# Four-layer graph network on one core: layer 2's last two gating tiles one by one, its last ELU from PSUM, W1 in halves, row exponentials and layer 3's score turns later

## The chip, the cores and the metric

The kernel runs on one core of one Trainium2 chip. The metric is device time in microseconds of one launch, the median of several runs, so less is better. A core has five engines, each with its own instruction queue, taken in order: TensorE (PE in the profile, its weight loads PEld), VectorE (DVE), ScalarE (ACT), GpSimd (POOL) and SyncE (SP), which here issues most of the DMAs. Engines wait for each other through semaphores. All data is float32. Each float32 product with a full tile shows up in the profile as two matmul records, a transposition as one.

## The reference, cut to what matters

x is 2708 x 256, adj is 2708 x 2708. Four layers each add a graph step and a feed-forward step to x. What the change touches lies in layer 2 and at the start of layer 3:

```python
# layer 2, graph step on xn = layernorm(x)
h = xn @ W.T
a_src = (h * attn_src).sum(-1);  a_dst = (h * attn_dst).sum(-1)
scores = a_src[None, :] + a_dst[:, None]
s = where(scores > 0, scores, 0.2 * scores) * mask          # mask = adj > 0
e = exp(s - max(s, axis=1)) * mask
x = x + elu(e / (sum(e, axis=1) + 1e-8) @ h)
# layer 2, feed-forward step on xn = layernorm(x)
logits = mean(xn, over all rows) @ Wr + br                  # one routing for all rows
weights = softmax(softmax(logits) * scale);  top 2 of 8 experts, softmax of the two
y = sum over the two experts of w_e * (gelu(xn @ W1[e] + b1[e]) @ W2[e] + b2[e])
x = x + layernorm(y + xn) * gamma + beta
# layer 3, graph step: four heads, score_l and score_r of xn @ W.T, softmax over neighbours
```

Since the routing of layer 2 depends on the mean over all rows, no expert can be chosen, and none of its weights loaded, before the last row's graph step is done.

## The kernel before, in words

The 2708 rows are 22 tiles of 128 rows, the last (number 21, `FULL`) with only 20. x stays in SBUF as `x[:, t, :]`. Eight PSUM banks have two roles in this part: three for short-lived results (`ps_tmp`) and five for accumulators (`ps_acc`); a new tile of a role waits until the one that had its bank is read.

**Layer 2's front** (lines 1570 to 1685) goes through the groups of tiles in `FOURS` (2, 4, 4, 4, 4, 4 tiles). `turned_up` adds what the layer before left in DRAM (`mine`, loaded by SP; added on DVE, from tile 14 on on POOL, line 1588), turns the tiles (PE, line 1596) and copies them to `xT4` (ACT, line 1598). `valued` multiplies with W and the two attention vectors (PE, line 267), copies the scores (ACT, line 1639) and puts `hh`, the scaled values, and exponentials of the scores. The scores along the row have to reach all partitions: `row_scores` turns them (PE, line 1497), copies them (ACT, line 1499) and writes them to DRAM (SP, line 1500); `row_factor` reads them back, broadcast to 128 partitions (SP, line 1504), and takes their exponential in place (ACT, `lnexp`, line 141). Since ACT's queue is in order, everything behind this exponential waits for the round trip through DRAM.

**Gating** (lines 1736 to 1782). The loop goes over batches of 5, 5, 5, 4 and 2 destination tiles. For each source tile j, one DVE instruction (line 1745) makes the weights `e` for all the batch's tiles, in one of four buffers; then PE adds `e.T @ hh[j]` to each tile's accumulator (line 1753; the 20 rows of tile 21 by `last_product`, line 313). Column 256 of `hh` yields the sum of weights. When a batch is through, `result` (line 1690) adds `rowe` to the sum, takes the reciprocal (DVE) and copies the scaled accumulator to `o` (ACT, line 1696). `grow` takes the ELU (relu and exponential on ACT, lines 1702 and 141; two additions on DVE, 1704 and 1705), and row statistics (DVE, 1707 and 1708; Ln and Exp on ACT). `turned` normalises to `xn` (ACT, 1717), turns it into `xnT` (PE, 1721), and its copies also sum the columns into `xsum` (ACT, 1726). These closings of a batch are handed out within the next batch's loop, one at every second j (line 1755).

**Routing** (lines 1786 to 1852). After the last batch of two tiles, PE adds bias and the column sums of the other 20 tiles to the logits, `grow` is run on the two tiles, and their share is added as a weighted sum (line 1798: x times the reciprocal deviation, one column). Then a chain of small DVE and ACT instructions picks two experts and their weights, and the two tiles are turned.

**Feed-forward** (lines 1912 to 2055). SP reads the experts' numbers from `ix`, and loads their W1 (128 x 2 x 512 each) and W2. Six parts of 512, 512, 512, 512, 384 and 276 rows follow: `units` makes the hidden layer of both experts (PE line 375, gelu on ACT line 377), `finish` normalises the part before, `outputs` multiplies with W2 (PE, line 1962), and `front` does layer 3's front for the part before: turn, project (line 267), copy values and scores (ACT, lines 2015 to 2018), and at its end turn the scores (`row_scores`, PE line 1497) and write them to DRAM. Layer 3's gating reads them later.

**What sets the order.** The program is written in the order of the source, and a scheduler then orders each engine's queue by its own estimate of times; `engine_after` and `after` add order by hand, tying an engine's instructions from one place on behind a named one. Each engine then runs its queue in that order.

Of the kernel before, what the change touches and what calls it, by code (L numbers as in the profile page):

```python
# [8 lines left out]
F32 = mybir.dt.float32  # L9
# [6 lines left out]
P = 128  # L16
N = 2708
D = 256
# [48 lines left out]
def adj_ffn4(ctx: ExitStack, tc: tile.TileContext, a: dict, out: bass.AP):  # L67
# [1438 lines left out]

    def row_factor(dst, kept, h, t0, n):

        row_read(dst, kept, h, t0, n)
        lnexp(dst, dst, AF.Exp, scale=0.8)  # L1510


# [4 lines left out]
    with tc.tile_pool(name="t3", reuse_waits="tile", bufs=1) as t3:  # L1517
# [25 lines left out]

        SUMMED = NT - 2
        xsum = tp.tile([P, DC, SUMMED], F32, name="xsum")

# [5 lines left out]
        with tc.tile_pool(name="g2", reuse_waits="tile", bufs=1) as gp:  # L1552
# [3 lines left out]
            Rb = gp.tile([P, NT * P], F32, name="Rb")  # L1556
            kept = tc.dram_tile([NT, 1, P], F32, name="rows2")

            fronts = (mybir.EngineType.PE, mybir.EngineType.DVE, mybir.EngineType.Activation)
# [10 lines left out]
            def turned_up(tiles):  # L1570

                n, t0 = len(tiles), tiles[0]
                adder = v if t0 < FOURS[4][0] else g
                xT = gp.tile([P, DC, W], F32, name="xT4", bufs=2)
                late = [t for t in tiles if t not in EARLY]
                if late:
                    o = gp.tile([P, 4, D], F32, name="mine", bufs=2)
                    for i in load_tiles(nc, o, late, given[1], t0):
                        behind(i, scattered["given1"])
# [46 lines left out]
            def scores_of(tiles):  # L1626
                sc = gp.tile([P, 4, 2], F32, name="sc", bufs=2)
                (v if tiles[0] < FOURS[2][0] else g).memset(sc, 0.0)
                return sc, []
# [26 lines left out]

            ahead, todo = [turned_up(FOURS[0])], list(FOURS[1:])
            for k in range(len(FOURS)):
                sc, t0, n = valued(*ahead.pop(0))
# [23 lines left out]
                if k > 0:  # L1683
                    row_scores(kept, sc[:, :n, 1], t0, n)
                row_factor(Rb[:, t0 * P : (t0 + n) * P], kept, 0, t0, n)

# [12 lines left out]
            def grow(t, q, o):  # L1699

                e = work.tile([P, D], F32, name="elu_e")[:q]
                s.activation(e, o, AF.Relu, scale=-1.0)
                lnexp(e, e, AF.Exp, scale=-1.0)
                v.scalar_tensor_tensor(x[:q, t, :], o, 0.0, x[:q, t, :], op0=ALU.max, op1=ALU.add)
                v.scalar_tensor_tensor(x[:q, t, :], e, -1.0, x[:q, t, :], op0=ALU.add, op1=ALU.add)
                st = small.tile([P, 6], F32, name="st")
                v.bn_stats(st[:q], x[:q, t, :])
                v.bn_aggr(mrs[:q, t, :], st[:q])
                lnexp(mrs[:q, t, 1:2], mrs[:q, t, 1:2], AF.Ln, bias=eps[:q])
                lnexp(mrs[:q, t, 1:2], mrs[:q, t, 1:2], AF.Exp, scale=-0.5)  # L1710
# [25 lines left out]
            t0, seen, todo = 0, 0, []  # L1736
            for n in (5, 5, 5, 4, 2):
                own = [(t, (t - t0) * P, P) for t in range(t0, t0 + n)]
                c0, w = t0 * P, n * P
                t0 += n  # L1740
                acc = [ps_acc() for _ in own]
                for j in range(NT):
                    r = P
                    e = gp.tile([P, 5 * P], F32, name="e", bufs=4)
                    i = v.scalar_tensor_tensor(e[:r, :w], Rb[:r, c0 : c0 + w], G[:r, j, :],  # L1745
                                           mask[:r, j, c0 : c0 + w], op0=ALU.max, op1=ALU.mult)
                    if c0 == 0 and j == 12:
                        spread = i.ins.name
                    for n, ((t, k, q), p) in enumerate(zip(own, acc)):
                        if j == FULL:  # L1750
                            last_product(p[:, : D + 1], n % 4, e, k, hh[:, FULL, :])
                        else:
                            te.matmul(p[:, : D + 1], lhsT=e[:, k : k + q], rhs=hh[:, j, :],  # L1753
                                      start=(j == 0), stop=False)
                    if j % 2 and j > 2 and todo:
                        todo.pop(0)()
                made = [result(t, q, p) for (t, k, q), p in zip(own, acc)]
                if c0 == 0:
# [14 lines left out]
                        ps_tmp(), es, lambda j, r: hh[:r, j, :], D + 1)))  # L1773
                if t0 == FULL:
                    break
                for it in made:
# [13 lines left out]
            for c in range(DC):  # L1790
                te.matmul(logits, lhsT=xb[:, c : c + 1].to_broadcast([P, P]), rhs=wr[:, c, :],
                          start=False, stop=False)
            for it in made:
                grow(*it)
            p = ps_tmp()
            for i, (t, q, _) in enumerate(made):
                for c in range(DC):
                    te.matmul(p[:, c : c + 1], lhsT=x[:q, t, c * P : (c + 1) * P],
                              rhs=mrs[:q, t, 1:2], start=(i + c == 0),
                              stop=(i == len(made) - 1 and c == DC - 1))  # L1800
            xb = gp.tile([P, DC], F32, name="xb", bufs=2)
# [48 lines left out]
            v.tensor_tensor(wts[:, 1, :], wts[:, 1, :], wts[:, 0, :], ALU.mult)  # L1850
            for it in made:
                turned(*it[:2])

# [58 lines left out]
        with tc.tile_pool(name="h2", reuse_waits="tile", bufs=2) as hp:  # L1912
# [4 lines left out]
            b1s = hp.tile([P, 2, H2C], F32, name="b1s", bufs=1)  # L1917
            chosen = [nc.values_load(ix[0:1, k : k + 1], engines=[mybir.EngineType.SP], min_val=0,
                                     max_val=E - 1,
                                     skip_runtime_bounds_check_because="the index of a one-hot's one")  # L1920
                      for k in range(2)]
            for k, e in enumerate(chosen):
                nc.sync.dma_start(w1[:, k], a["L2_ffn_W1"][bass.ds(e, 1)].rearrange(
                    "e (c p) h -> p (e c) h", p=P))
            for k, e in enumerate(chosen):
# [103 lines left out]

            was = None  # L2030

            parts = CHUNKS[:-2] + [(CHUNKS[-2][0], 3 * P), (CHUNKS[-2][0] + 3 * P, W + CHUNKS[-1][1] - 3 * P)]
            for c0, w in parts:
                own = tiles_of(c0, w)
                end = c0 + w == N
                hT, i = units(c0, w)
                if end:


                    pin(i.ins.name)  # L2040
                    rows_of(0, "both")
                    last_mask()
                    factors(0, was[0][0][0])
                if was is not None:
                    at_once(finish(*was, end))
                y = ypool.tile([P, 4, D], F32, name="y", bufs=2)
                outputs(own, hT, y)
                if was is not None:
                    at_once(front(was[0]))
                    for t in range(NT) if was[0][0][0] == 0 else ():  # L2050
                        r = rows(t)
                        g.tensor_copy(mask[:, t, t * P : t * P + r], diag[:, t, :r])
                if end:
                    factors(was[0][0][0], own[0][0])
                was = (own, y)
# [262 lines left out]
```

## Time and profile before

| | us |
|---|---|
| median of three runs (1900.36 to 1915.36) | 1911.79 |
| the profiled execution's own time | 1882.29 |
| its span in the profile | 1880.6 |
| PE busy in the span | 1820.4 |
| DVE busy | 1076.1 |
| ACT busy | 656.0 |
| POOL busy | 387.3 |
| mean clock granted to PE, share of full | 0.985 |

By stage, in us from the span's start: layer 2's front from about 1063 to 1095, its gating from 1095 to 1308.5, the routing to 1324, the feed-forward step to 1508, layer 3 to the end. In a line of the timeline the first number is the start, the second the duration (of all where x says more than one), then engine, source line, operation, what is written and from what, the shape, and in brackets how long the engine stood idle before and what ended that. A line of the waits gives engine and line, who released it, the total in us, how often and the longest. Durations are those of one execution.

### The profile page before, as it was taken

How to read it: one execution, taken by the hardware profiler on the slowest of the kernel's cores; microseconds unless marked ns; L12 is line 12 of the kernel's file. 1: busy time of each engine (PE TensorE's matmuls, PEld its weight loads, DVE VectorE, ACT ScalarE, POOL GpSimd, SP SyncE). 2: the span in 40 equal slices, each digit the busy share in tenths (PEclk: the TensorE clock that was granted, in tenths of full speed). 3: DMA queues.
4: the chain of work that ended last, by engine and by line, in shares of the span. 5: the costliest groups of instructions: out<-in, count | busy, mean ns of one | idle time of the engine just before them, and what ended most of it. 6: DMA issues, size and time to landing. Idle time of an engine off the chain costs nothing. (4 is left out here: it accounts for less than half of the span.)

```text
span 1880.6 us, 25848 instructions
## 1 busy us (share of the span) xinstructions
PE 1820.4 (97%) x9453; PEld 1335.0 (71%) x9453; DVE 1076.1 (57%) x2468; ACT 656.0 (35%) x1474; POOL 387.3 (21%) x460
## 2 busy tenths in 40 slices
PE   8999999999999999999999899998899999999998
PEld 7888788888888888888788788887566733233344
DVE  7687863444333525354642465555445498888877
ACT  8868742222222303113232323223223551132232
POOL 0014254333331001403547310000000100011020
PEclk9999999999998999999999999999899999999999
DMA  8535657877873554544775430000101000022120
GB/s 269 157 104 161 225 177 283 336 301 281 305 272 108 165 150 119 146 113 130 218 235 166 140 70 7 1 1 1 45 1 34 18 1 24 23 28 35 26 35 18
DMA packets 92494, 231.63 MB, mean 123 GB/s; under 512 B 18207, under 2 KB 48967, under 8 KB 84936
## 3 DMA queue, kind: packets, MB, share of 16 engines
q1 hardware_dynamic: 70792, 183.28, 29.8%
q0 software_dynamic: 21568, 46.61, 8.9%
q8 instruction: 78, 1.28, 0.3%
q14 instruction: 56, 0.46, 0.1%
HBM read 218.39 MB, written 30.80 MB: 133 GB/s over the span
## 5 line engine op out<-in xcount | busy, mean ns | idle before, releaser
L2190 DVE SCALAR_TENSOR_TENSOR e<-arena,G,mask 128x1024 f32<-128x1024 f32 (+1 forms) x252 | 275.1, 1151 | 34.1 <-PE den L2227 33.2
L2219 PE MATMUL num<-e,wh 128*64 128x512 f32 (+4 forms) x1056 | 214.1, 549 | 0.7 <-ACT L_gnn_W L1499 0.3
L1753 PE MATMUL ps_acc<-hh,e 128*128 128x257 f32 x882 | 199.2, 382 | 1.7 <-ACT o L1696 1.7
L1025 PE MATMUL acc<-msg,wt 128*128 128x256 f32 x882 | 197.8, 381 | 1.5 <-DVE wt L975 1.2
L1421 PE MATMUL acc<-sup,adrow 128*128 128x256 f32 x882 | 198.3, 382 | 0.7 <-DMA adrow<-in_adjT 0.4
L1421 PEld LDWEIGHTS acc<-sup,adrow 128*128 128x128 f32 x882 | 165.1, 190 | 28.4 <-issue 5.5
L1753 PEld LDWEIGHTS ps_acc<-hh,e 128*128 128x128 f32 x882 | 164.0, 191 | 29.0 <-ACT o L1696 4.3
L1025 PEld LDWEIGHTS acc<-msg,wt 128*128 128x128 f32 x882 | 165.5, 191 | 26.7 <-DVE wt L975 1.8
L615 PE MATMUL ps_acc<-xTs,wa 128*128 128x256 f32 (+1 forms) x768 | 169.9, 374 | 2.8 <-DVE xTs L605 2.7
L617 ACT ACTIVATE hTs<-ps_acc,wa 128x256 f32<-128x256 f32 (+1 forms) x192 | 88.8, 464 | 237.7 <-PE yacc L649 155.6
L649 PE MATMUL yacc<-wb,hTs 128*128 128x256 f32 x736 | 170.6, 384 | 0.1
L615 PEld LDWEIGHTS ps_acc<-xTs,wa 128*128 128x128 f32 x768 | 137.2, 191 | 29.0 <-DVE xTs L605 5.1
L2219 PEld LDWEIGHTS num<-e,wh 128*64 128x64 f32 (+1 forms) x1056 | 70.2, 136 | 122.7 <-issue 105.4
L649 PEld LDWEIGHTS yacc<-wb,hTs 128*128 128x128 f32 x736 | 138.8, 192 | 18.1 <-DVE ys L651 0.5
L1745 DVE SCALAR_TENSOR_TENSOR e<-Rb,G,mask 128x640 f32<-128x640 f32 (+2 forms) x110 | 85.0, 774 | 90.5 <-PE ps_acc L1753 90.4
L1386 DVE TENSOR_SCALAR mask<-adrow 128x1024 uint8<-128x1024 f32 (+1 forms) x66 | 41.6, 630 | 124.1 <-DMA adrow<-in_adjT 123.7
L2227 PE MATMUL den<-e,wh 128*32 128x512 f32 (+4 forms) x1056 | 112.2, 546 | 0.0
L221 ACT COPY xT<-ps_tmp 128x256 f32<-128x256 f32 x76 | 26.8, 366 | 199.1 <-PE ps_tmp L220 198.7
L782 PE MATMUL yacc<-wb,hTs 128*128 128x256 f32 x384 | 90.0, 390 | 0.0
L975 DVE SCALAR_TENSOR_TENSOR wt<-adrow,wt 128x640 f32<-128x640 f32 (+3 forms) x67 | 71.2, 1065 | 25.1 <-ACT wt L141 24.8
L2227 PEld LDWEIGHTS den<-e,wh 128*32 128x32 f32 (+1 forms) x1056 | 33.2, 109 | 73.6 <-issue 69.5
L537 POOL DMA_INDIRECT given<-ys,xs x46 | 65.3, 1420 | 84.0 <-DVE ys L652 68.2
(487 smaller groups left out, 2632.6 us busy)
## 6 DMA issues: line engine op xcount, KB each, us to landing
adhalf<-in_adjT SPq DMA_DIRECT2D x42, 677.0 KB
wb<-in_L_ffn_W2p SPq DMA_DIRECT2D x24, 1152.0 KB
wb<-in_L_ffn_Wdp SPq DMA_DIRECT2D x24, 1152.0 KB
wa<-in_L_ffn_W1b SPq DMA_DIRECT2D x24, 1028.0 KB
adrow<-in_adjT SPq DMA_DIRECT2D x42, 512.0 KB
adrow<-in_adjT SPq DMA_DIRECT2D x42, 320.0 KB
adrow<-in_adjT SPq DMA_DIRECT2D x21, 576.0 KB
adrow<-in_adjT SPq DMA_DIRECT2D x21, 448.0 KB
```

The costliest lines, as they stand in the source:

```text
L615: i = te.matmul(p[:, f % 2, : m * P], lhsT=w1[:, c, f * P : (f + 1) * P], rhs=xT[:, c, : m * P], start=(c == 0), stop=(c == DC - 1))
L617: s.activation(hT[:, f, : m * P], p[:, f % 2, : m * P], AF.Gelu, bias=bias[:, f : f + 1])
L649: te.matmul(q[:, k, :], lhsT=hT[:, f, k * P : (k + 1) * P], rhs=w2[:, f, :], start=(f == 0), stop=(f == HC - 1))
L782: te.matmul(q, lhsT=hT[:, f, :], rhs=w2[:, f, :], start=(f == 0), stop=(f == HC - 1))
L975: v.scalar_tensor_tensor(wt, ad, 1.0, wt, op0=ALU.is_lt, op1=ALU.mult)
L1025: te.matmul(p[:q, n - pair[0], :], lhsT=wt[:, k : k + q], rhs=msg[:r, j, :], start=(j == 0 and n == pair[0]), stop=(j == FULL - 1 and n == ...
L1421: te.matmul(p[:q, n - pair[0], :], lhsT=ad[:, k : k + q], rhs=sup[:, jj, :], start=(jj == 0 and n == pair[0]), stop=(jj == FULL - 1 and n ...
L1745: i = v.scalar_tensor_tensor(e[:r, :w], Rb[:r, c0 : c0 + w], G[:r, j, :], mask[:r, j, c0 : c0 + w], op0=ALU.max, op1=ALU.mult)
L1753: te.matmul(p[:, : D + 1], lhsT=e[:, k : k + q], rhs=hh[:, j, :], start=(j == 0), stop=False)
L2190: v.scalar_tensor_tensor(e[:, :w], slow[:, m % 2, k, :w], G[:, j, 2 * pair + k, :], mask[:, j, c0 : c0 + w], op0=ALU.max, op1=ALU.mult)
L2219: te.matmul(num[k * DK : (k + 1) * DK, hf, :q], lhsT=wh[some, j, 2 * pair + k, :DK], rhs=e[some, :q], start=(j == 0), stop=(j == FULL), ti ...
L2227: te.matmul(den[z * Q : (z + 1) * Q, :q], lhsT=wh[some, i, 2 * pair + k, DK : DK + 1] .to_broadcast([some.stop - some.start, Q]), rhs=e[so ...
```

## The change

- The row exponential is taken one group later: `row_factor` is gone; after the next group's `row_scores`, `factors_of` takes the exponential of the group before, tied behind ACT's last instruction.
- The buffers of the front get a pool of their own, which is closed after the front; its room goes to 22 kept tiles of weights `e_last` (128 x 256).
- The batches are 5, 5, 5, 4, 1 and 1. The weights of both single tiles are made in one instruction for each source tile: 18 of them within the four-tile batch, four right after it. The single passes read them; closings are handed out at j = 4, 9, 14 and 19 of a single pass.
- `SUMMED` is 21: only the last full tile (20) is added to the mean by the weighted sum.
- The last tile's ELU reads the accumulator in PSUM: the sum and reciprocal are taken with a minus sign, ACT's relu scales with it, and DVE takes min(-v, 0) and subtracts it from x. The rest of `grow` is now `normed_by`.
- The first expert's W1 is loaded in two halves of 256 columns, with the second expert's number read after them.
- A part's last step of `front`, the turn of the scores, is emitted after the next part's `units`, with PE tied behind its last product; the last part's is run at once.

```diff
-    def row_factor(dst, kept, h, t0, n):
-        row_read(dst, kept, h, t0, n)
-        lnexp(dst, dst, AF.Exp, scale=0.8)
...
-        SUMMED = NT - 2
+        SUMMED = NT - 1
...
+            def factors_of(dst):
+                had, first = last_of(fronts), len(nc.cur_bb.bb.instructions)
+                lnexp(dst, dst, AF.Exp, scale=0.8)
+                engine_after(first, mybir.EngineType.Activation, had[mybir.EngineType.Activation])
...
-                row_factor(Rb[:, t0 * P : (t0 + n) * P], kept, 0, t0, n)
+                for f in factor:
+                    factors_of(f)
+                factor = [Rb[:, t0 * P : (t0 + n) * P]]
+                row_read(factor[0], kept, 0, t0, n)
+            factors_of(factor[0])
...
+            def weigh_last():
+                both_last.append(pair_pool.tile([P, 2 * P], F32, name="e_last", bufs=NT))
+                return weigh(both_last[-1], len(both_last) - 1, PAIR * P, 2 * P)
...
-            for n in (5, 5, 5, 4, 2):
+            for n in (5, 5, 5, 4, 1, 1):
+                single = t0 - PAIR
...
+                    if single >= 0:
+                        if len(both_last) < NT and single == 0:
+                            weigh_last()
+                        e = both_last[j]
+                    else:
+                        e = gp.tile([P, 5 * P], F32, name="e", bufs=4)
+                        i = weigh(e, j, c0, w)
+                        if t0 == PAIR and j > 3:
+                            after(weigh_last(), i.ins.name)
...
-                    if j % 2 and j > 2 and todo:
+                    if (j in (4, 9, 14, 19) if single >= 0 else j % 2 and j > 2) and todo:
                         todo.pop(0)()
...
-            for it in made:
-                grow(*it)
+            t, p = FULL - 1, acc[0]
+            rs = small.tile([P, 1], F32, name="rs")
+            v.scalar_tensor_tensor(rs, p[:, D : D + 1], -1.0, rowe[:, t, :], op0=ALU.mult,
+                                   op1=ALU.subtract)
+            v.reciprocal(rs, rs)
+            e = work.tile([P, D], F32, name="elu_e")
+            s.activation(e, p[:, :D], AF.Relu, scale=rs)
+            lnexp(e, e, AF.Exp, scale=-1.0)
+            o = gp.tile([P, D], F32, name="o", bufs=6)
+            v.tensor_scalar(o, p[:, :D], rs, 0.0, op0=ALU.mult, op1=ALU.min)
+            v.tensor_tensor(x[:, t, :], x[:, t, :], o, ALU.subtract)
+            normed_by(t, P, e)
...
+                for h0 in ((0, H2 // 2) if k == 0 else (0,)):
+                    h1 = H2 if k else h0 + H2 // 2
+                    nc.sync.dma_start(w1[:, k, :, h0:h1], a["L2_ffn_W1"][bass.ds(e, 1), :, h0:h1]
+                                      .rearrange("e (c p) h -> p (e c) h", p=P))
...
                 hT, i = units(c0, w)
+                if scored is not None:
...
+                    at_once(scored)
+                    engine_after(at, mybir.EngineType.PE, done)
+                    scored = None
...
-                    at_once(front(was[0]))
+                    scored = front(was[0])
+                    for _ in range(len(was[0]) + 1):
+                        next(scored)
+                    if end:
+                        at_once(scored)
```

## The prediction

> **What bounds the kernel now.** I read the page's busy shares first, then TensorE's waits, then the timeline of each place that the diff touches.
>
> ```profile
> PE 1820.4 (97%) x9453; PEld 1335.0 (71%) x9453; DVE 1076.1 (57%) x2468; ACT 656.0 (35%) x1474; POOL 387.3 (21%) x460
> ```
> TensorE (PE) is the bound nearly everywhere: 1880.6 - 1820.4 = 60 us of the span are left for all its idle time. The change removes no sizeable PE work, so it can win only parts of that idle time. Who ends it (line, releaser, total us, times, longest):
>
> ```profile
> PE ps_tmp L1497 <- issue: 5.1, 5, 1.1
> PE ps_tmp L1798 <- ACT mrs L141: 4.0, 1, 4.0
> ...
> PE ps_tmp L1596 <- ACT xT L1598: 3.4, 1, 3.4
> ...
> PE ps_acc L1753 <- ACT o L1696: 1.7, 3, 0.8
> ...
> PE ps_tmp L375 <- DMA w<-in_L_ffn_W: 0.8, 1, 0.8
> ...
> PE ps_tmp L1721 <- ACT xn L1717: 0.6, 1, 0.6
> ```
> These six are the waits that the edits aim at. The first is named "issue", but the timeline (start, duration, engine, line) shows that the turn of the scores starts when ScalarE (ACT) has written the last of them:
>
> ```profile
> 1384.01 2.24 PE L267 MATMUL ps_tmp<-w_l,xT 128*128 128x264 f32 x8
> 1387.00 0.28 ACT L2018 ACTIVATE sc<-ps_tmp,rs_y 128x4 f32<-128x4 f32 x1
> 1387.39 0.27 PE L1497 MATMUL ps_tmp<-ident,sc 128*16 128x128 f32 x1 [1.14 <-issue]
> ```
> In layer 2's front, ACT stands 4.29 us for a row's round trip through DRAM, and PE then lacks the copies queued behind it; GpSimd's (POOL's) two adds run in the same gap:
>
> ```profile
> 1076.42 2.48 POOL L1588 TENSOR_TENSOR x<-x,mine 128x512 f32<-128x512 f32 x2 [6.61 <-DMA mine<-given]
> 1076.76 0.42 ACT L141 ACTIVATE Rb<-Rb 128x256 f32<-128x256 f32 x1 [4.29 <-DMA Rb<-rows]
> ...
> 1079.33 1.09 PE L1596 MATMUL ps_tmp<-ident,x 128*128 128x128 f32 x4 [3.36 <-ACT xT L1598]
> ```
> After the last gating product a chain over two tiles runs with PE idle:
>
> ```profile
> 1308.69 0.16 DVE L1693 TENSOR_TENSOR rs<-ps_acc,rowe 128x1 f32<-128x1 f32 x1 [2.75 <-PE ps_acc L313]
> 1310.92 1.03 DVE L1705 SCALAR_TENSOR_TENSOR x<-elu_e,x 128x256 f32<-128x256 f32 x2 [0.16 <-ACT elu_e L141]
> 1313.36 1.86 PE L1798 MATMUL ps_tmp<-mrs,x 128*128 128x1 f32 x8 [4.04 <-ACT mrs L141]
> 1324.04 1.19 PE L375 MATMUL ps_tmp<-arena,w 128*128 128x512 f32 x1 [0.82 <-DMA w<-in_L_ffn_W]
> ```
> The windows by time (us, then busy time by engine, third number from the end the clock granted to PE) show a second price of a long gap:
>
> ```profile
> 1074.00:1076.00 2.00, 1.91 (x12) 1.03 (x10) 2.00 (x7) 0.00 (x0) 0.00 (x0) 1.00 0.80 255
> 1079.30:1080.30 1.00, 0.97 (x5) 1.00 (x6) 1.00 (x3) 0.52 (x2) 0.00 (x0) 0.50 0.36 39
> 1084.30:1085.30 1.00, 1.00 (x4) 0.86 (x3) 0.12 (x1) 0.26 (x1) 0.77 (x3) 0.65 0.61 117
> ```
> The clock is halved after the 3.36 us gap, and whole again only some 5 us into steady work.
>
> **What the Trainium skill says.** "TensorE: Matmul & The Clock Gate", section "The HAM clock gate": an idle window of about 3.4 us halves PE's clock, about as long a busy one restores it, and the window runs free. The trace agrees in kind: gaps of 0.6 to 1.2 us leave the clock whole, one of 1.75 (at 253.3) too, but those of 2.10 (at 1036.1) and 2.26 (at 992.3) already halve it. "PSUM — Partial Sum Buffer", section "PSUM bank collisions raise a hardware error": ScalarE and VectorE may not read one bank at once. This decides a step below: in the changed program VectorE's (DVE's) read of the accumulator waits for ACT's, so the two reads add. The trace of before has no such pair. [...]Here 512 KB of W1 took 4.1 us from issue (1319.92) to the product that waits for it (1324.04), and nearly nothing moved in its first two us.
>
> **The change part by part**, against the profiled execution: span 1880.6, its own time 1882.29; the runs' median is 1911.79 (1900.36 to 1915.36), so the profiled execution was 1.5% quicker than the median. The difference in us is carried over.
>
> (e) Four of layer 3's five score turns move behind the next 32 hidden products (the fifth, at the end, stays). Each then finds its scores written, and the hidden products start when the front's last product ends. Gain: the four gaps, 1.14 + 1.08 + 1.08 + 0.92 = 4.2 us. The turns still cost their 0.11 each. Cover: the 32 products, 7.6 to 13.9 us, against 1.1 us of ACT work. Queues that they are moved past: ACT's copy (0.25) now follows the eight gelus, where only the row's DMA write waits for it; SP's writes come up to 14 us later and the first reader's exponential runs at 1492, 50 us after the second write; POOL's clear of the last score buffer falls behind 0.98 + 5.25 us of mask copies (1490.7 to 1497), still ahead of its writer at 1504.4. The last turn's copy adds 0.25 to ACT's run at 1491, where PE later waits 0.94 for ACT. Without the cover: if the hidden products lacked a free bank of the three, they would wait for the same reads. The third-last bank is the one copied at 1384.66, so they don't. Value 4.2, bounds 3.2 to 4.6.
>
> (b) Last chain, one tile and from PSUM. Before, from 1308.69 to 1313.36: 4.67 us. Now: sum and reciprocal to ACT's start 0.45 (as 1308.69 to 1309.14); the relu from PSUM 0.47 (an `o` from PSUM takes 0.46 to 0.47); then DVE's own PSUM read, held until then, 0.54 (a tensor_scalar of 256 from PSUM at 1078.47), the subtraction 0.46, with the exponential (0.41) beside them; the add of e 0.46; statistics 0.46; their sum up to ACT's start 0.19; Ln 0.32 and Exp 0.24. Sum 3.6, gain 1.05. The weighted sums L1798 are two products (four records) instead of four: 1.86 becomes 0.93. Together 2.0. Tile 19's part of xsum and its turn now come before; of the last `turned` half the turns and copies go, which stand beside DVE's routing (PE waits 3.25 us for `wd` there) and gain nothing. Bounds: 1.0, if PSUM reads on both engines cost more, to 2.6, if DVE's two steps hide.
>
> (a) Gating by ones. PE's products are the same 42 of 0.434 us. DVE's 22 weights of 0.48 move: 18 into the four-tile pass, where one row takes PE 1.74 us and DVE 0.75 + 0.48 with about 1 us free per row; the first rows also hold the older tiles' closing, but following DVE's new order its e stays over 1.5 us ahead. So this costs nothing; its cover gone, it would cost PE up to 0.5 us a row. The 0.36 us wait for an accumulator goes, as the fifth bank is free. But the first turn still follows eleven products: PE arrives 0.9 us earlier, at 1291.6, at a chain (four tiles' ELU and statistics on ACT and DVE in pairs) that I follow to 1292.7 (before: 1293.10). Gain 0.4. Then two short waits appear: 0.2 for the third tile, and 0.35 for tile 19, whose chain (4.35 us with its `xn`) meets only nine products (3.9). Two added turns cost 0.26. Value -0.4, bounds -1.3 to +0.8.
>
> (c) W1's first half. PE could start at 1323.2 and waited 0.82 for 512 KB. Data flowed at some 350 GB/s (estimate from the DMA rate in that stretch), so 256 KB less is about 0.7 us. Rows halve to 1 KB each, so less: value 0.6, bounds 0 to 0.82. Queued behind the extra issue (0.4 us on SP) are W1's second expert and W2: needed 7 and 14 us after the start. The second half is needed 3.5 us after the first.
>
> (d) Row exponentials. In the program's order only the first moves (128x256, 0.42 us), behind the next group's score copy; the other five keep their place. ACT no longer stands until 1076.76; its two copies end by about 1076.5. Next late: the same PE turn waits for POOL's first add, 1076.42 + 1.24 = 1077.66, which hangs on a DMA. The gap falls from 3.36 to about 1.75 us: gain 1.6. If the clock stays whole, more; but the next tiles' adds (POOL, 1083.63 to 1085.03, behind a load that SP issues at 1078.93 after POOL) hold the turns that ran at 1087.05, so at most 2.0 is kept. Value 1.7, bounds 0.5 to 2.2.
>
> Sum: 4.2 + 2.0 - 0.4 + 0.6 + 1.7 = 8.1 us. The profiled execution would become 1874.2, the median 1911.8 - 8.1 = **1904**.
>
> **Rivals.** (1) *Waits that take the removed ones' place*: hidden products wait for banks (e gives 1), POOL holds the front (d 0.5), two reads of PSUM collide (b 1): 1 + 1 - 0.4 + 0.6 + 0.5 = 2.7 us, 1909. For it: ACT feeds all of these; against it: bank by bank the reads end early. (2) *The passes by ones also run smoother*: +0.8 there, 2.6 for b, 4.6 for e, 0.8 for c, 2.2 for d: 11 us, 1901. For it: DVE is freed of the weights just there. (3) *Slower*: PE's clock falls in the passes by ones. PE stands 1.05 us at the first turn by my count; from 1.75 to 2.1 us on the clock halves, and with more waits at each later turn PE may not look busy enough to get it back (after a gap of 1.71 us at 595.9 it stayed halved for 9 us). Then the 31 products left take 13.5 us more; with 1 us of waiting 14.5 against 8.1: 6.4 slower, 1918. It decides at 0.7 us more wait than I count. Against it: products fill the gaps there.
>
> **How the numbers follow.** Forecast (effect 5 to 10 us) 0.6, rival 1 0.2, rival 2 0.14, rival 3 0.06. The effects with their bounds span 1901 to 1909; the runs before lie 11 below to 4 above their median, which a median of few runs shares, so I give 1894 to 1913. One per cent, 19 us, is about what a measurement of this kernel can tell from no change. No case gains that much; scatter alone can show it: faster 0.11, same 0.85, slower 0.04.
>
> **What would show it.** In the profile after: no wait at the score turns but one of about 0.9; the wait at the weighted sums near 3.0; the front's near 1.75, and whether the clock halves; W1's wait near 0.2; new waits of 0.2 to 1.1 at the turns within the passes by ones. Wrong if PE stands over 2 us at the first turn of those, if hidden products show a wait for ACT, or if the front's gap ends later than 1078.

## The result, and the profile after

The changed kernel takes 1904.33 us (median of 22 runs, 1896.79 to 1910.26), the kernel before 1910.59 us in the same comparison (22 runs). The ratio is 0.9967 with a 95% interval of 0.9955 to 0.9979: 6.3 us less, between 4.0 and 8.6. Measured a second time against runs of its own, it gave 0.9975 (0.9961 to 0.9988).

The profiled execution of the changed kernel has a span of 1903.4 us, longer than the 1880.6 of the page before. That isn't the change. Layer 2's front, the first place that the diff touches, starts at 1092.46 us instead of 1062.95, and the 29.5 us lie in layers 0 and 1. The level differs between sets of runs: the kernel before itself took 1880.9 us in one later set and 1905.9 in another, on another chip. So the traces are compared from layer 2's front on, to the end of TensorE's last matmul, some 6 us before the span ends. A second profile of the changed kernel (further down) repeats each of these stretches within 0.7 us.

| stretch (us) | before | after | difference | predicted |
|---|---|---|---|---|
| layer 2's front, to the first gating product | 32.53 | 30.67 | -1.86 | -1.7 (d) |
| gating, to the sum `rs` of the last chain | 213.21 | 215.09 | +1.88 | +0.4 (a) |
| from there to the first hidden product | 15.35 | 12.80 | -2.55 | -2.6 (b, c) |
| feed-forward, to layer 3's first product | 183.65 | 179.10 | -4.55 | -4.2 (e) |
| layer 3 | 367.13 | 367.16 | 0.0 | 0 |
| all from layer 2's front | 811.87 | 804.82 | -7.05 | -8.1 |

First the page's busy shares after:

```profile
PE 1829.0 (96%) x9449; PEld 1338.0 (70%) x9449; DVE 1074.8 (56%) x2469; ACT 656.5 (34%) x1475; POOL 390.2 (20%) x460
```

And TensorE's waits after (engine, tile, line, releaser: total us, times, longest):

```profile
PE ps_tmp L1840 <- ACT mrs L141: 3.3, 1, 3.3
...
PE ps_tmp L1593 <- POOL x L1585: 1.8, 1, 1.8
PE ps_tmp L1736 <- ACT xn L1732: 1.6, 2, 1.2
...
PE ps_tmp L1593 <- POOL sc L1625: 1.2, 2, 0.9
...
PE ps_tmp L1497 <- issue: 0.9, 1, 0.9
```

Of five waits at the turn of the scores (5.1 us) one is left. The wait at the weighted sums is 3.3 instead of 4.0. The front's 3.4 us wait for ScalarE is a 1.8 us wait for POOL. The wait at the turns within gating, L1736, has grown from 0.6 to 1.6.

The front in the timeline, answering the prediction's fourth block of lines (start, duration, engine, line):

```profile
1107.19 0.66 PE L1593 MATMUL ps_tmp<-ident,x 128*128 128x128 f32 x4 [1.82 <-POOL x L1585]
...
1109.02 3.22 PE L267 MATMUL ps_acc<-w_l,xT 128*128 128x258 f32 x14
1113.15 1.17 PE L1593 MATMUL ps_tmp<-ident,x 128*128 128x128 f32 x6 [0.91 <-POOL sc L1625]
```

Before, the 14 records of the second line took longer:

```profile
1082.14 4.63 PE L267 MATMUL ps_acc<-w_l,xT 128*128 128x258 f32 x14
```

Two windows of the same place, answering its sixth block (the clock is third from the end):

```profile
1107.46:1108.46 1.00, 0.87 (x7) 0.46 (x5) 1.00 (x5) 0.57 (x1) 0.91 (x1) 1.00 0.00 0
1109.46:1110.46 1.00, 1.00 (x6) 0.89 (x5) 0.19 (x3) 0.64 (x3) 0.00 (x0) 1.00 0.63 182
```

After the 1.82 us gap the clock stays at 1.00. The 14 records (seven products) take 3.22 us, where at half clock they took 4.63. But then the next turns wait 0.91 us for POOL: its third add starts only at 1111.84, when the rows that it adds have been loaded (POOL stood 3.47 us for them). A part of what the clock gives is lost again.

The passes by ones (the two gating passes over a single tile each), the last chain and the start of the hidden products:

```profile
1314.68 5.05 PE L1786 MATMUL ps_acc<-hh,e_last 128*128 128x257 f32 x22
1320.95 0.33 PE L1736 MATMUL ps_tmp<-ident,xn 128*128 128x128 f32 x1 [1.23 <-ACT xn L1732]
...
1326.70 0.70 PE L313 MATMUL ps_acc<-hh,e_last 20*128 20x257 f32 x2
...
1331.89 0.33 PE L1736 MATMUL ps_tmp<-ident,xn 128*128 128x128 f32 x1 [0.33 <-ACT xn L1732]
...
1342.05 0.98 PE L1840 MATMUL ps_tmp<-mrs,x 128*128 128x1 f32 x4 [3.33 <-ACT mrs L141]
...
1351.02 1.22 PE L375 MATMUL ps_tmp<-arena,w 128*128 128x512 f32 x1
```

The same place in the kernel before:

```profile
1286.80 0.70 PE L1753 MATMUL ps_acc<-hh,e 128*128 128x257 f32 x2
1287.86 4.61 PE L1753 MATMUL ps_acc<-hh,e 128*128 128x257 f32 x20 [0.36 <-ACT o L1696]
1293.10 0.33 PE L1721 MATMUL ps_tmp<-ident,xn 128*128 128x128 f32 x1 [0.63 <-ACT xn L1717]
...
1307.95 0.70 PE L313 MATMUL ps_acc<-hh,e 20*128 20x257 f32 x4
```

Here the loss can be read. PE has done eleven products and stands 1.23 us before the first turn, which comes 6.27 us after the start of the pass; in the kernel before it came 6.30 us after it (1293.10 - 1286.80). From the start of these passes to the sum `rs` it takes 23.54 us (1314.68 to 1338.22), before 21.89 (1286.80 to 1308.69). The first hidden product starts without a wait for W1.

### The profile page after: what moved, and what is told of

It is laid out like the page before. It is cut to its first block, busy times and chain, and to the rows that moved or that the text cites. A ratio compares the mean times of both kernels' runs of the same rounds, so it can differ in the third digit from the quotient of the medians.

```text
span 1903.4 us, 25846 instructions
## 1 busy us (share of the span) xinstructions
PE 1829.0 (96%) x9449; PEld 1338.0 (70%) x9449; DVE 1074.8 (56%) x2469; ACT 656.5 (34%) x1475; POOL 390.2 (20%) x460
## 3 DMA queue, kind: packets, MB, share of 16 engines
q8 instruction: 78, 1.28, 0.3%
## 5 line engine op out<-in xcount | busy, mean ns | idle before, releaser
L1421 PE MATMUL acc<-sup,adrow 128*128 128x256 f32 x882 | 202.2, 388 | 0.1
L1786 PE MATMUL ps_acc<-hh,e 128*128 128x257 f32 x798 | 179.5, 381 | 1.4 <-ACT o L1707 1.4
L1786 PEld LDWEIGHTS ps_acc<-hh,e 128*128 128x128 f32 x798 | 148.3, 190 | 26.1 <-ACT o L1707 3.5
L1755 DVE SCALAR_TENSOR_TENSOR e<-Rb,G,mask 128x640 f32<-128x640 f32 (+1 forms) x88 | 74.4, 847 | 77.0 <-PE ps_acc L1786 76.9
```

Source lines behind the costliest of these rows:

```text
L1421: te.matmul(p[:q, n - pair[0], :], lhsT=ad[:, k : k + q], rhs=sup[:, jj, :], start=(jj == 0 and n == pair[0]), stop=(jj == FULL - 1 and n ...
L1755: return v.scalar_tensor_tensor(e[:, :w], Rb[:, c0 : c0 + w], G[:, j, :], mask[:, j, c0 : c0 + w], op0=ALU.max, op1=ALU.mult)
```

## The experiments

All kernels below compute the same as the changed kernel. "The passes" is the stretch from the first product of the passes by ones to `rs`; "the last chain" is the one from `rs` to the weighted sums. Where no ratio is given, the kernel ran once, for its profile.

**The score turns (e), undone and alone.** First, the changed kernel without that edit:

```diff
-                    scored = front(was[0])
-                    for _ in range(len(was[0]) + 1):
-                        next(scored)
-                    if end:
-                        at_once(scored)
+                    at_once(front(was[0]))
```

> The changed kernel with the score turns back ahead of the hidden products (edit e undone). Theory (the turns' waits were worth their length): the stretch from the first hidden product to layer 3's first product grows from 179.1 us to about 183.5 (+4.4), four waits of 0.9 to 1.1 us come back at the turn, and the ratio to the kernel before goes from 0.997 to about 0.999. Rival (the feed-forward stretch became shorter for another reason, for instance W1's halves or the other buffers): it stays within 0.5 us of 179.1 us. Rival (the four gaps were half hidden): +1 to +2.5 us.

The second has the same lines the other way round, with the block `if scored is not None` behind `units`, in the kernel before.

> The kernel before with the score turns moved behind the next hidden products (edit e alone). Theory: the stretch from the first hidden product to layer 3's first product falls from 183.65 us to about 179.2 (-4.4), all other stretches stay within 0.3 us; ratio to the kernel before about 0.9977. Rival (the gain needs the other edits): less than 2 us falls away there.

TensorE's waits at the turn in the kernel with the turns back:

```profile
PE ps_tmp L1497 <- issue: 5.1, 5, 1.1
```

And in the kernel before with nothing but the turns moved:

```profile
PE ps_tmp L1497 <- issue: 0.9, 1, 0.9
```

With the turns back the feed-forward stretch is 183.76 us (+4.66), and the ratio to the kernel before 0.9995 (0.9983 to 1.0006). With the turns alone it is 178.84 us (-4.81), and the ratio 0.9970 (0.9961 to 0.9979). So edit e does the work in the runs: without it the rest can't be told from no change, and alone it gives as much as the whole. The stretch lies between 178.4 and 179.7 us in the twelve profiles with the turns moved, and at 183.65 and 183.76 in the two without.

**Passes by ones and last chain (a, b), undone together.**

```diff
-            for n in (5, 5, 5, 4, 1, 1):
+            for n in (5, 5, 5, 4, 2):
...
-        SUMMED = NT - 1
+        SUMMED = NT - 2
...
-            t, p = FULL - 1, acc[0]
...
-            normed_by(t, P, e)
+            for it in made:
+                grow(*it)
```

> The changed kernel with layer 2's last two tiles again in one pass and the last ELU over both (edits a and b undone, the others kept). Theory (the passes by ones give back all that the shorter last chain gains): the stretch from the first gating product to the first hidden product is 227.8 us, within 0.4 us of the changed kernel's 227.9. Rival (the prediction's working: passes by ones cost 0.4, the last chain gains 2.0): 229.5 us. Rival (the passes by ones cost far less, and the 1.9 us lost there are of this one trace): 231 us or more.

From the first gating product to the first hidden product: 227.67 us, against 227.89 in the changed kernel. The ratio to the kernel before is 0.9972 (0.9962 to 0.9981). The two edits together give nothing: what the last chain and the sums behind it gain (from `rs` on 14.46 us here, 12.80 there: 1.66), the passes by ones lose. The prediction's working, with 1.6 us of net gain, falls.

**The row exponential (d), undone.**

```diff
-                for f in factor:
-                    factors_of(f)
-                factor = [Rb[:, t0 * P : (t0 + n) * P]]
-                row_read(factor[0], kept, 0, t0, n)
-            factors_of(factor[0])
+                factor = Rb[:, t0 * P : (t0 + n) * P]
+                row_read(factor, kept, 0, t0, n)
+                lnexp(factor, factor, AF.Exp, scale=0.8)
```

> The changed kernel with the exponential of each row's factors again right behind its row's read (edit d undone). Theory (ScalarE's stand for the row and the halved clock after it made the difference): layer 2's front, 30.67 us in the changed kernel, becomes 32.5 again; TensorE's 3.4 us wait at the second tiles' turn is back, ended by ScalarE, and the granted clock halves behind it. Rival (the front became shorter by other buffers or by the loads' timing, not by the exponential): the front stays within 0.4 us of 30.7.

The timeline of that kernel's front:

```profile
1075.51 1.09 PE L1593 MATMUL ps_tmp<-ident,x 128*128 128x128 f32 x4 [3.38 <-ACT xT L1595]
...
1078.32 4.58 PE L267 MATMUL ps_acc<-w_l,xT 128*128 128x258 f32 x14
```

Two windows of the same place:

```profile
1075.82:1076.82 1.00, 1.00 (x5) 0.91 (x4) 1.00 (x4) 0.36 (x3) 0.00 (x0) 0.50 0.31 99
...
1079.82:1080.82 1.00, 1.00 (x3) 0.81 (x3) 0.74 (x2) 0.40 (x2) 1.00 (x2) 0.50 0.76 158
```

The gap is back, ended by ScalarE, and the clock is halved for the 14 records: 4.58 us. The front takes 32.79 us (+2.12). It was 30.4 to 30.9 us in all eleven profiles with the edit, and 32.5 to 32.8 in the three without.

**W1 in one load (c undone).**

```diff
-                for h0 in ((0, H2 // 2) if k == 0 else (0,)):
-                    h1 = H2 if k else h0 + H2 // 2
+                for h0 in (0,):
+                    h1 = H2
```

> The changed kernel with the first expert's W1 in one load (edit c undone). Theory (the first half arrives in time, the whole does not): from the sum of the last chain to the first hidden product 12.8 us become 13.6, with a wait of about 0.8 for the load, as in the kernel before. Rival (TensorE reaches the hidden products late enough for the whole matrix, since the load is issued earlier relative to it in the changed kernel): 12.8, no wait.

The timeline of this kernel, from the weighted sums to the first hidden product:

```profile
1313.87 0.61 PE L1840 MATMUL ps_tmp<-mrs,x 128*128 128x1 f32 x4 [3.33 <-ACT mrs L141]
...
1323.08 2.90 PE L375 MATMUL ps_tmp<-arena,w 128*128 128x512 f32 x3 [0.54 <-DMA w<-in_L_ffn_W]
```

The same of a second profile of the changed kernel (its expectation stands further down):

```profile
1336.14 0.61 PE L1840 MATMUL ps_tmp<-mrs,x 128*128 128x1 f32 x4 [3.33 <-ACT mrs L141]
...
1344.72 2.93 PE L375 MATMUL ps_tmp<-arena,w 128*128 128x512 f32 x3
```

From `rs` to the first hidden product this kernel takes 13.05 us: only 0.25 more than the changed kernel's first profile, and neither of the expected numbers. The reason is in the line of the weighted sums, not in the load. Here they took 0.61 us, in the first profile 0.98, behind the same gap of 3.33 us: there the clock had been halved by then (0.58 from 1341.9 to 1343.2), here not yet (0.80 in the like window). The second profile of the changed kernel has 0.61 as well, and 12.41 us. Against that one the whole load costs 0.64 us, of which 0.54 are shown as a wait. With the pass of two the stretch is 14.46 us with the halves (the pair kernel), 15.05 and 15.35 without (the turns alone, the kernel before): 0.6 to 0.9 us for the same edit.

**Where the passes by ones lose.** The first kernel ties the turns behind later products: the first turn of each pass comes three products later, the last of tile 19's pass stays where it was. The second also shares a 20-row product, and has `FULL` in place of 19 in `LATE`, so that this last turn is tied behind the shared product. With `last_product` of tile 19 at the end of its pass, tile 20's is made beside it in another row group, as the first of its sum:

```diff
+            LATE = ((13, 15, 17, 19), (11,))
...
-                    if (j in (4, 9, 14, 19) if single >= 0 else j % 2 and j > 2) and todo:
+                    if (j in LATE[single] if single >= 0 else j % 2 and j > 2) and todo:
+                        at = len(nc.cur_bb.bb.instructions)
                         todo.pop(0)()
+                        if single >= 0:
+                            engine_after(at, mybir.EngineType.PE, prod.ins.name)
```

> The changed kernel with every turn in the passes by ones three products later and nothing else. Theory (of x7's 1.5 us, the waits at the turns gave about 0.9 net, since 0.84 came back as a wait for ScalarE's copies at the second turn, and the shared 20-row product the other 0.6): from the start of the passes by ones to the sum of the last chain 22.65 us, where the changed kernel has 23.54 and x7 22.02. Rival (the 20-row product costs nothing of its own and the turns gave it all): 22.0. Rival (the turns gave nothing): 23.3.

```diff
                             last_product(p[:, : D + 1], n % 4, e, k, hh[:, FULL, :])
+                            if single == 0:
+                                ahead_acc = ps_acc()
+                                prod = te.matmul(ahead_acc[:, : D + 1], lhsT=e[Q : Q + LAST, P : 2 * P],
+                                          rhs=hh[Q : Q + LAST, FULL, :], start=True, stop=False,
+                                          tile_position=(Q, 0))
```

> The changed kernel with two edits in the passes by ones: every turn three products later, so that TensorE doesn't arrive before the first turn's input, and the 20-row product that ends tile 19's pass side by side with tile 20's, which begins with it instead of ending with it. Theory (the loss in the passes by ones is 1.2 + 0.3 us of waits at the turns and some 0.5 us for a lone 20-row product): from the start of the first pass by ones to the sum of the last chain 23.5 becomes 21.5 us (-2.0), the wait at the first turn is below 0.3. Rival (the waits only move to the next turns, because ScalarE and VectorE set the pace of the closing chains): within 0.5 us of 23.5. Rival (the clock falls): more than 25.

The timeline of the second, with the turns and the shared product:

```profile
1288.98 0.33 PE L1736 MATMUL ps_tmp<-ident,xn 128*128 128x128 f32 x1
...
1291.02 0.44 PE L1736 MATMUL ps_tmp<-ident,xn 128*128 128x128 f32 x2 [0.84 <-ACT arena L1741]
...
1293.89 0.48 PE L313 MATMUL ps_acc<-hh,e_last 20*128 20x257 f32 x1
1293.90 0.48 PE L1788 MATMUL ps_acc<-hh,e_last 20*128 20x257 f32 x1
```

The passes took 22.26 us with later turns alone and 22.02 with both, where the changed kernel has 23.54. The wait at the first turn and the one for tile 19 are gone in both. But a new wait of 0.83 and 0.84 us stands at the second turn: ScalarE does the third tile's scaled input before it copies the first tile's turn out of PSUM, and no bank is free. The later turns gave 1.28 us, more than the 0.9 expected, and the shared product 0.24, less than 0.6; of the 2.0 us expected of both, 1.5 came. The end of the pass did get shorter by 0.62 us (from the last 14 records of products to `rs` 3.25 instead of 3.87), but the turn that moved behind the product is followed by a gap of 0.3 us of its own. The ratio with both is 0.9956 (0.9939 to 0.9973).

The next kernel takes that kernel and holds ScalarE to an order:

```diff
                         grow(*it)
+                        mid = len(nc.cur_bb.bb.instructions)
                         turned(*it[:2], n)
+                        if PAIR - 4 <= it[0] < PAIR:
+                            copied.append(last_of(fronts)[mybir.EngineType.Activation])
+                            if len(copied) > 2:
+                                engine_after(mid, mybir.EngineType.Activation, copied[-3])
```

> The kernel of x7 with ScalarE held to an order: the third tile's scaled input of the turn comes behind the copies of the first tile's turn. Theory (in x7 the second turn waited 0.84 us for those copies, which stood behind that input): the wait goes, and from the start of the passes by ones to the sum of the last chain 22.02 us become 21.3; ratio to the kernel before about 0.995. Rival (TensorE then waits at the third turn for the later input instead): 22.0 again.

The timeline of its first and second turn:

```profile
1288.61 0.33 PE L1736 MATMUL ps_tmp<-ident,xn 128*128 128x128 f32 x1
...
1289.96 0.44 PE L1736 MATMUL ps_tmp<-ident,xn 128*128 128x128 f32 x2 [0.15 <-ACT arena L1741]
```

The passes take 21.33 us: the wait at the second turn is 0.15, and none appears at the third. From layer 2's front to the end it is 801.84 us, and the ratio to the kernel before 0.9955 (0.9943 to 0.9967). The passes by ones don't have to lose: mended, they take 0.56 us less than the pass of two did (21.89).

**The last ELU from PSUM (a part of b).** One kernel forms it from a copy in SBUF, still with one tile; the other is the kernel with ScalarE's order, with both PSUM reads on VectorE:

```diff
-            s.activation(e, p[:, :D], AF.Relu, scale=rs)
-            lnexp(e, e, AF.Exp, scale=-1.0)
-            o = gp.tile([P, D], F32, name="o", bufs=6)
-            v.tensor_scalar(o, p[:, :D], rs, 0.0, op0=ALU.mult, op1=ALU.min)
-            v.tensor_tensor(x[:, t, :], x[:, t, :], o, ALU.subtract)
-            normed_by(t, P, e)
+            o = gp.tile([P, D], F32, name="o", bufs=6)
+            s.activation(o, p[:, :D], AF.Copy, scale=rs)
+            grow(t, P, o)
```

> The changed kernel with the last ELU, still of one tile, formed from a copy of the scaled sums in SBUF as all other tiles' are (the part of edit b that reads PSUM twice undone, the single tile kept). Theory (the two PSUM reads of ScalarE and VectorE add up, and tile 19's own chain, which has the copy, takes 3.06 us from its sum to its logarithm against 3.25 of the last tile): from the sum of the last chain to the weighted sums 3.84 us become 3.58, faster by 0.26; edit b's gain is then the single tile's alone. Rival (the reading from PSUM saves the copy, as the prediction's 3.6 us against one step more has it): 4.1 or more.

```diff
-            s.activation(e, p[:, :D], AF.Relu, scale=rs)
+            v.tensor_scalar(e, p[:, :D], rs, 0.0, op0=ALU.mult, op1=ALU.max)
```

> The kernel of x10 with both PSUM reads of the last ELU on VectorE, the exponential's first, so that neither engine waits for the other's read. Theory (what costs in the changed kernel is the hand-over between two engines that read one bank): from the sum of the last chain to the weighted sums 3.84 us become 3.65. Rival (the reads of PSUM themselves cost, on whatever engine): 3.8 or more.

The timeline of the last chain in the changed kernel, from PSUM, with POOL's work beside it:

```profile
1338.22 0.16 DVE L1828 SCALAR_TENSOR_TENSOR rs<-ps_acc,rowe 128x1 f32<-128x1 f32 x1 [4.38 <-PE ps_acc L313]
...
1339.17 0.48 DVE L1835 TENSOR_SCALAR o<-ps_acc,rs 128x256 f32<-128x256 f32 x1 [0.60 <-ACT elu_e L1832]
1339.26 2.22 POOL L1928 COPY corner<-mask 20x384 uint8<-20x384 uint8 x4
1339.69 0.42 DVE L1836 TENSOR_TENSOR x<-x,o 128x256 f32<-128x256 f32 x1
1340.22 0.54 DVE L1720 SCALAR_TENSOR_TENSOR x<-elu_e,x 128x256 f32<-128x256 f32 x1
```

And in the kernel with the copy:

```profile
1333.81 0.16 DVE L1828 TENSOR_TENSOR rs<-ps_acc,rowe 128x1 f32<-128x1 f32 x1 [4.38 <-PE ps_acc L313]
...
1334.86 2.24 POOL L1923 COPY corner<-mask 20x384 uint8<-20x384 uint8 x4
...
1335.66 0.70 DVE L1720 SCALAR_TENSOR_TENSOR x<-elu_e,x 128x256 f32<-128x256 f32 x1 [0.47 <-ACT elu_e L141]
```

The last chain is 3.85 us with the copy, 3.83 without and 3.77 with both reads on VectorE. For the copy neither the theory (3.58) nor the rival (4.1 or more) holds, and 3.77 lies between 3.65 and 3.8. Reading PSUM twice gains nothing and costs next to nothing. With the copy the last addition does start earlier, 1.85 us behind `rs` instead of 2.00, but it takes 0.70 us instead of 0.54, and 0.42 for tile 19, whose chain meets no work of POOL. The Trainium skill ("SBUF — State Buffer", section "Who interferes with whom") says that a VectorE instruction with two inputs in SBUF contends with a GpSimd instruction that reads SBUF. The traces agree. Taken one by one, POOL's four copies and VectorE's additions take longer when they start second. In all fourteen profiles an addition that starts well within a copy ends 0.28 us after that copy (at 1340.76 behind a copy's end at 1340.48 in the changed kernel, at 1336.36 behind 1336.09 with the copy in SBUF). A copy of POOL that starts within the subtraction of 1339.69, which keeps its 0.42, takes 0.68; the last of the four, with no addition beside it, 0.42. So with the copy in SBUF the last addition starts earlier, but 0.07 us behind the start of one of POOL's copies, and loses what it gained. The cause rests on this timing: no run moved POOL's copies away, and what the chain would take without them isn't measured.

**Both mendings together, and the changed kernel again.** The first has the lines of the last two diffs that concern the order and the copy, the second no edit.

> The kernel of x10 with x8's copy: the passes by ones mended and the last ELU from SBUF. Theory: x10's 801.8 us from layer 2's front to the end fall by 0.26 to 801.6, passes 21.3, last chain 3.58; ratio to the kernel before about 0.995. Rival (the copy costs as in x8's rival): 802.2.

> The changed kernel itself once more. Theory (the 29.5 us by which its first profile is later at layer 2's front lie in layers that the change doesn't touch, and are of that execution): the front starts near 1061 us as in the other kernels' profiles, all later stretches repeat within 0.5 us, ratio to the kernel before about 0.9965. Rival (the change itself makes layers 0 and 1 slower): the front starts near 1090 again.

The first: passes 21.33, last chain 3.85, 802.31 us from layer 2's front (the rival's 802.2), ratio 0.9959 (0.9946 to 0.9972). Its median in this set is 1898.60 us, the changed kernel's 1901.97. The copy isn't worth its line; the kernel with ScalarE's order alone is the shortest by its trace, and the ratios can't tell the two apart. The changed kernel again: 804.75 us from layer 2's front (804.82 in the first profile), gating to `rs` 215.10 (215.09). Its feed-forward stretch took 179.71 us (179.09), a little outside the 0.5 us that I had allowed. Its front started at 1086.85 us, not near 1061, so my number for it missed. But in this set the unchanged kernel took 1905.94 us too, 25 more than in the two sets in which the eight profiled kernels, with all or some of the edits, had their front at 1058.8 to 1064.4 (1880.9 and 1881.5). The rival, that the change slows layers 0 and 1, doesn't fit that.

## Why the prediction was right or wrong

- **The time.** 1904 was predicted and 1904.3 measured. It rests on a sum of 8.1 us of gain, where the traces show 7.05 and the runs 6.3 (4.0 to 8.6). That the two times meet this closely is luck in part: the median of before, 1911.8 in the three runs that the prediction had, is 1910.6 in 22, and that offsets 1.2 of the 1.8 us by which the gain fell short. Of the signs it named for being wrong none appeared: TensorE stood 1.23 us at the first turn (named: over 2), the hidden products show no wait for ScalarE, and the front's gap ends 14.7 us after the front's start (named: later than 15.05).
- **(e) 4.2 us: right in its mechanism, somewhat small.** 4.55 in the pair of traces, 4.66 undone, 4.81 alone, the last two over its bound of 4.6. The prediction added up the gaps in brackets. These begin at the end of the record before, which the profile models: it lasts 0.39 us there, while such records follow each other after 0.22 when nothing waits. Counted from start to start, the four waits are 0.17 us longer each, 4.9 us in all. The named cover held: the 32 records (16 products, not 32) hide the copy, and no wait for a bank appeared. The one turn expected to stay is the one left, with 0.9 us.
- **(d) 1.7 us: right, with its mechanism.** The gap fell to 1.82 us (predicted 1.75), ended by POOL's add as named; the clock stayed whole; POOL held later turns. 1.86 came out, 2.12 undone.
- **(b) 2.0 us: nearly.** 1.66 by the pair kernel: 0.84 in the chain (predicted 1.05) and 0.82 behind it (0.93 for the halved sums). What the chain takes more than predicted lies for the most part in the last two steps of VectorE beside POOL's copies (from start to start 0.53 and 0.57 us, predicted 0.46 each). The step "DVE's own PSUM read, held until then" was right: it starts at 1339.17, when ScalarE's read ends at 1338.67 + 0.47. The chain was worth its one tile, not its reading from PSUM.
- **(c) 0.6 us: right.** 0.64 against the changed kernel at the same clock, one execution each; 0.6 to 0.9 with the pass of two. The wait expected at 0.2 is none.
- **(a) -0.4 us: the term that was mis-sized.** It measured -1.88, outside its bounds of -1.3 to +0.8. Three of its steps failed. The chain "that I follow to 1292.7", 5.9 us after the start of the pass, took 6.27 us, as long as before (6.30): its end is set by the ELU and statistics of four tiles, and not by when PE arrives. PE came 0.63 us earlier (predicted 0.9) and only waited longer: 0.4 us of gain that didn't come. "PE's products are the same": the second pass has a 20-row product of its own, for which I wrote no price. Its two records take 0.70 us, as long as the four records of the two products in the kernel with the pair (0.70 as well); from its start to the next turn it is 0.62 (1326.70 to 1327.32). "So this costs nothing": one turn in the four-tile batch comes 0.24 us later with the kept weights beside it. The third tile's 0.2 us wait didn't come. Predicted 0.4, + 0.4 + 0.6 + 0.24 - 0.2: 1.44 of 1.88. Most of the other 0.44 is in delays that the brackets don't show: counted from start to start, the wait for tile 19 is 0.49 us instead of 0.33, and two turns (1321.88 and 1324.59) come 0.22 and 0.14 us late behind ScalarE's copies, where the kernel before has one such delay of 0.13.
- **The rivals.** The clock didn't fall in the passes by ones (1.00 throughout, with 1.23 us of wait at the first turn, below the 1.75 I had named). Smoother passes were possible, but only with the turns moved and ScalarE's order held. Banks did take away a part once turns were moved (0.84 us), in the changed kernel only the 0.36 us just named. The halved clock after the gap at 595.9 lasts until about 610, some 13 us and not 9.

The excess in e and d (0.35 + 0.16 us) covers a third of what a was short (1.48), b and c together come within 0.05 of their sum, and the scatter of the runs (15 us from the lowest to the highest of before) hides the rest. The predicted total is no proof of its parts; only the stretches show that one of them had the wrong size.

## What to carry to other kernels

An engine that is let off earlier gains nothing if the next thing it needs is set by a chain on other engines: count from the chain's start, not from the engine's arrival. Splitting a batch repeats its ends; price the short product at the end of a pass and every turn by their own rows, not by their share in a larger group. A gap in brackets before a record of TensorE leaves out a part of the wait, here some 0.16 us each: count from start to start. When the work of an engine is moved, look at what stands in the queue of the engine that frees its buffers: here one order on ScalarE was worth 0.7 us.

## What the runs showed of the hardware

- The clock of TensorE after one and the same gap is not always the same. Seven profiles have a gap of 3.33 to 3.35 us before the weighted sums of one tile. In four of them these took 0.98 to 1.01 us, in three 0.60 to 0.61; there the clock fell a little later (0.50 from 1315.0 to 1318.0 in the kernel with W1 in one load). The Trainium skill ("TensorE: Matmul & The Clock Gate", section "The HAM clock gate") says that the window runs free, which would give that. For a comparison it means 0.4 us that no edit made.
- A pass's 20-row product, two records, takes 0.62 us alone; two side by side in two row groups take 0.64 (1293.89 to the turn at 1294.53), and eight records in four groups 0.65 (1314.03 to 1314.68). Its price is nearly independent of how many share it. The Trainium skill ("TensorEngine Tiling (Array Packing)", section "Key Properties") says that changing the tiling mode drains TensorE; a price that hardly depends on the number of records would fit that, but no run here separates the drain.
- The level of a whole run differed by 25 us between sets of runs of the same kernel (1880.9 and 1905.9 us), four times what the change is worth; in the profiles of the changed kernels it lies before layer 2's front. The sets of 1880.9 and 1881.5 us ran on two chips, that of 1905.9 on a third; no run separates the chip from the time. Only runs of one set can be compared.
